# Summing the expert output biases on GpSimd, with logits in column tiles, gathers by pairs and the flag inside the stream

## The chip, the cores, the metric

The kernel runs on one core of one Trainium2 chip, in fp32. The metric is the device time in microseconds of one execution; medians of several executions are given. Every execution quoted here counted as fast (undisturbed).

PE is TensorE, PEld its weight loads, DVE VectorE, ACT ScalarE, POOL GpSimd. The traces name a program line with L; lines move a little from kernel to kernel. The granted clock is the share of its full clock that PE was given; 0.50 is called half rate. Tiles that start with ps lie in PSUM: psh is the output of an expert's first or second layer, psy of a combine, psr holds the routing logits, pswt the transposed routing weights, psbo the biases, pss the window attention's logits, psa a gather; psrt and lgT belong to the changed logits, wbe and wb to the changed biases, pw holds the window weights.

## The reference, cut to what matters

The input has 32 x 128 tokens of 256 channels. Layer 0 is attention over all tokens; layer 1 is a windowed attention (24 neighbours) and a mixture of eight experts, all of them used for every token and weighted by a softmax:

```python
def _L1_ffn_ref(x, Wr, br, W1, ..., W2, ..., Wo, bo):
    feat = jnp.mean(x, axis=0)
    w = jax.nn.softmax(feat @ Wr + br, axis=-1)              # routing weights, tokens x 8
    h = jnp.einsum('bfd,edh->bfeh', x, W1) + b1
    h = jax.nn.relu(_bn(h, g1, be1, m1, v1))
    h = jnp.einsum('bfeh,ehk->bfek', h, W2) + b2
    h = jax.nn.relu(_bn(h, g2, be2, m2, v2))
    y = jnp.einsum('bfeh,ehd->bfed', h, Wo) + bo             # bo: 8 x 256
    return jnp.einsum('bfed,fe->bfd', y, w)                  # so sum_e w_e * bo_e is added
```

## The kernel before

Layer 1 is one hand-ordered stream (the scheduler keeps the program's order on every engine). A "piece" is the matmuls of an expert's first layer, of its second layer, or of a combine; there are 193, one per slot. The side work of a group of four token tiles (one block of 512 tokens; eight groups) is put into slots between the pieces, and a new group starts every 24 slots (one period). In each slot VectorE's, ScalarE's and GpSimd's steps (the `POSTS`) are issued first, then TensorE's side steps, then the piece. Two PSUM banks (`ps_x`) serve all side steps in turn.

```python
        def gather(i, early=False):                    # window-weighted sum of tile i
            acc = bank(f"psa{i}", early)[:, : D + 1]
            nc.tensor.matmul(acc, lhsT=pws[i][:, EDGE : EDGE + P], rhs=xl[:, i % NRING, :], ...)
            if i:                                      # 32 rows of the tile before
                nc.tensor.matmul(acc[:EDGE], lhsT=pws[i - 1][P - EDGE :, EDGE + P :],
                                 rhs=xl[P - EDGE :, (i - 1) % NRING, :], ...)
            if i + 1 < NTILE:                          # 32 rows of the tile after
                nc.tensor.matmul(acc[P - EDGE :], lhsT=pws[i + 1][:EDGE, :EDGE],
                                 rhs=xl[:EDGE, (i + 1) % NRING, :], ...)
        # ... cut ...
        def route(b, early=False):                     # routing logits: 8 columns out
            ...
            for r in range(TPB):
                for c in range(2):
                    nc.tensor.matmul(lg[:, r, :], lhsT=xfT[:, c, r * P : (r + 1) * P],
                                     rhs=Wr[:, c, :], start=(c == 0), stop=(c == 1))
        # ... routed, route_exp, route_norm: the softmax on VectorE and ScalarE, cut ...
        def turn_routes(b):                            # weights, transposed: 8 rows
            ps = bank(f"pswt{b}", False)
            for r in range(TPB):
                nc.tensor.transpose(ps[:E, r * P : (r + 1) * P], blk[b][1][:, r, :], ident)
        # ... turned_routes: VectorE copies them to wT, cut ...
        def biases(b):                                 # sum_e w_e * bo_e as 8-row matmuls
            for r2 in range(TPB // 2):
                ps = bank(f"psbo{b}_{r2}", False)
                for k in range(2):
                    r = 2 * r2 + k
                    nc.tensor.matmul(ps[:, k * D : (k + 1) * D],
                                     lhsT=wT[:, r * P : (r + 1) * P], rhs=bo, start=True, stop=True)
        def biased(b):                                 # VectorE adds them to the tokens
            for r2, ps in enumerate(banks.pop(("b", b))):
                t = h1[b * TPB // 2 + r2]
                nc.vector.tensor_tensor(t, t, ps.rearrange("p (k d) -> p k d", k=2), op=ALU.add)
        # ... cut: the slots of one group ...
            put(26, route, g); put(27, routed, g); put(28, route_exp, g); put(29, route_norm, g)
            put(31, turn_routes, g); put(32, turned_routes, g)
            put(34, biases, g); put(35, biased, g)
        # ... cut ...
        START = 26                                     # the slot of the first piece
        # ... cut: the stream; after it, with nothing beside them: ...
        in_range(wf, ok, rs1, 1.0e-34, 1.0e17)         # four VectorE steps each
        in_range(wf, ok, G.rearrange("p k c -> p (k c)"), 1.0e-15, 1.0e15)
        nc.tensor.matmul(n_ok, lhsT=ok, rhs=ones_m[:, :1], start=True, stop=True)
        nc.vector.tensor_scalar(flag, n_ok, P - 0.5, None, op0=ALU.is_lt)
```

Every engine then reads the flag and branches: if a check failed, a general kernel does the work again.

## Time and profile before

| | before |
|---|---|
| median | 1620.54 us (1619.7 to 1621.57, 3 executions) |
| profiled execution | span 1620.3 us, mean granted PE clock 0.988 |
| first expert matmul, end of the last combine | 800.7, 1610.2 us |
| PE busy | 1579.3 us, 97% |

In the timeline a row is: start, length, engine, line, operation, output <- inputs, shape, number of instructions, and in square brackets the idle time before it and what ended it. In the view of stretches a row is: stretch, its length, then the busy time (and number of instructions) of PE, PEld, DVE, ACT and POOL, the granted PE clock, the DMA share and GB/s. The timelines are in the prediction. The view of stretches over one period before:

```profile
1114.81:1218.26 103.45, 103.16 (x374) 63.98 (x374) 30.45 (x81) 32.19 (x45) 2.85 (x4) 1.00 0.03 11
```

### The profile page before, as it was taken

What the parts mean: (1) busy time and instruction counts of PE and PEld (TensorE: products, weight loads), DVE (VectorE), ACT (ScalarE), POOL (GpSimd) and SP (SyncE); (2) the same over time, 40 slices, a digit from 0 to 9 for tenths busy, and PEclk for the clock granted to TensorE, in tenths of its full rate; (3) what the DMA queues carried; (4) which work ended last, traced back from release to release, by engine and by line L of the source; (5) the groups of instructions that cost most, each with busy time, mean ns of one, the idle gap of its engine ahead of it and who ended that gap; (6) DMA issues with size and microseconds to landing.
All of it is one profiled execution on the core that took longest, in us unless ns stands there. A gap on an engine that the chain in (4) does not pass through costs nothing.

```text
span 1620.3 us, 20972 instructions
## 1 busy us (share of the span) xinstructions
PE 1579.3 (97%) x8636; PEld 770.1 (48%) x8636; DVE 830.5 (51%) x1117; ACT 810.7 (50%) x1005; POOL 70.5 (4%) x230
## 2 busy tenths in 40 slices
PE   7999999999999999998899999999999999999997
PEld 5663332222222222223565656656656566565654
DVE  4543668888898898998523223233232232323212
ACT  3226778888888888885323322333233232332321
POOL 0002100000000000000100000000000000000000
PEclk9999999999999999999999999999999999999998
DMA  4200000000000000003200000000000000000000
GB/s 115 58 1 16 16 9 15 9 8 8 2 8 9 1 8 8 1 8 119 71 1 0 26 1 13 14 0 27 0 8 19 1 14 0 0 14 0 14 0 15
DMA packets 30251, 26.58 MB, mean 16 GB/s; under 512 B 7818, under 2 KB 28168, under 8 KB 30148
## 3 DMA queue, kind: packets, MB, share of 16 engines
q1 hardware_dynamic: 28600, 23.68, 5.1%
q10 hardware_dynamic: 1548, 1.48, 0.4%
q8 instruction: 70, 1.15, 0.3%
q14 instruction: 33, 0.27, 0.1%
HBM read 20.71 MB, written 4.44 MB: 16 GB/s over the span
## 4 chain that ended last, share of the span: by engine, by line
PE 96%; DVE 2%; ACT 1%; DMA 0%; issue 0%; ACTq 0%; DVEq 0%
PE psh L1746 28%; PE s L1232 19%; PE av L1269 16%; PE psy L1771 14%; PE z L1254 3%; PE psk L1078 2%; PE pso L1415 2%; PE psk L1489 2%; PE psv L1104 2%; PE psq L1119 2%; PE pss L1514 1%; PE psa L1563 1%; PE psr L1616 1%; PE psa L1558 1%; PE psbo L1667 1%; PE ptf L1599 0%
## 5 line engine op out<-in xcount | busy, mean ns | idle before, releaser
L1241 ACT ACTIVATE pt<-s 128x1024 f32<-128x1024 f32 (+2 forms) x576 | 515.9, 951 | 113.0 <-PE s L1232 102.9
L1284 DVE TENSOR_TENSOR pt<-pt,pt 128x2048 f32<-128x2048 f32 x210 | 481.1, 2291 | 24.6 <-PE av L1269 4.6
L1754 ACT ACTIVATE h<-psh,bshift,bscale 128x512 f32<-128x512 f32 x256 | 198.8, 777 | 551.9 <-PE psh L1746 551.9
L1232 PE MATMUL s<-QT,KT 32*128 32x512 f32 (+3 forms) x2304 | 338.2, 606 | 3.0 <-ACT pt L1241 2.2
L1780 DVE SCALAR_TENSOR_TENSOR h<-psy,w,h 128x256 f32<-128x256 f32 x256 | 112.1, 480 | 407.8 <-PE psy L1771 407.8
L1269 PE MATMUL av<-pt,V 128*32 128x512 f32 (+3 forms) x2304 | 286.9, 570 | 0.0
L1746 PE MATMUL psh<-xfT,W_sb 128*128 128x512 f32 x512 | 238.6, 610 | 0.0
L1771 PE MATMUL psy<-Wo_sb,h 128*128 128x256 f32 x1024 | 233.1, 380 | 0.4 <-ACT h L1754 0.4
L1746 PE MATMUL psh<-h,W_sb 128*128 128x512 f32 x512 | 231.9, 595 | 0.0
L1232 PEld LDWEIGHTS s<-QT,KT 32*128 32x128 f32 x2304 | 117.8, 183 | 227.1 <-issue 118.5
L1771 PEld LDWEIGHTS psy<-Wo_sb,h 128*128 128x128 f32 x1024 | 192.6, 190 | 41.1 <-ACT h L1754 10.0
L1746 PEld LDWEIGHTS psh<-xfT,W_sb 128*128 128x128 f32 x512 | 97.2, 195 | 115.6 <-issue 115.2
L1746 PEld LDWEIGHTS psh<-h,W_sb 128*128 128x128 f32 x512 | 95.4, 190 | 100.3 <-issue 97.6
L1269 PEld LDWEIGHTS av<-pt,V 128*32 128x32 f32 x2304 | 46.9, 108 | 195.5 <-issue 181.2
L1254 PE MATMUL z<-pt,ones_m 128*32 128x512 f32 (+3 forms) x624 | 61.9, 469 | 2.2 <-DVE pt L1284 2.2
L1246 POOL MEMSET pt<- 64x256 f32 x64 | 19.9, 311 | 646.8 <-ACT pt L1241 569.5
L907 POOL TENSOR_TENSOR xr<-xr,outb 128x512 f32<-128x512 f32 x16 | 20.2, 1270 | 493.5 <-DMA xr<-in_x_dram 454.2
L1291 DVE COPY ctx<-av 128x512 f32<-128x512 f32 x16 | 11.1, 691 | 59.1 <-PE av L1269 59.1
L1415 PE MATMUL pso<-woT,big_t 128*128 128x256 f32 x128 | 33.4, 411 | 5.1 <-DVE big_t L1325 5.1
L1254 PEld LDWEIGHTS z<-pt,ones_m 128*32 128x32 f32 x624 | 18.6, 110 | 31.5 <-issue 23.0
L1677 DVE TENSOR_TENSOR h<-h,psbo 128x512 f32<-128x512 f32 x16 | 11.0, 688 | 44.0 <-PE psbo L1667 44.0
L1489 PE MATMUL psk<-big_t,Ksb 128*128 128x256 f32 x128 | 30.6, 381 | 2.4 <-ACT big_t L1470 2.4
(150 smaller groups left out, 830.5 us busy)
## 6 DMA issues: line engine op xcount, KB each, us to landing
xg<-in_x_dram SPq DMA_DIRECT2D x32, 128.0 KB
xr<-in_x_dram SPq DMA_DIRECT2D x16, 256.0 KB
W_sb<-in_L_ffn_W_dram SPq DMA_DIRECT2D x16, 256.0 KB
out_dram<-h SPq DMA_DIRECT2D x16, 256.0 KB
rec<-rd SPq DMA_DIRECT2D x60, 64.0 KB
Wo_sb<-in_L_ffn_Wo_dram SPq DMA_DIRECT2D x8, 256.0 KB
in_w_n<-in_L_conv_in_w_dram ACTq DMA_DIRECT2D x1, 512.0 KB
wq_n<-in_L_conv_wq_dram ACTq DMA_DIRECT2D x1, 256.0 KB
```

The lines of the kernel that those rows point to most:

```text
L1078: nc.tensor.matmul(ps, lhsT=wKT[:, c, m * P : (m + 1) * P], rhs=hT[:, c, :], start=(c == 0), stop=(c == 1),)
L1232: nc.tensor.matmul(s[hh // 2][:, hh % 2, lo:], lhsT=KT[rows, g, i * P : (i + 1) * P], rhs=QT[rows, g, b * BLK + lo : (b + 1) * BLK], start ...
L1241: nc.scalar.activation(pt[:, 2 * hp : 2 * hp + 2, lo:], s[hp][:, :, lo:], AF.Exp, scale=SCALE)
L1254: nc.tensor.matmul(zs_ps[k][HD * hh : HD * (hh + 1), lo:], lhsT=ones_m[:, :HD], rhs=pt[:, hh, lo:], start=start, stop=stop,)
L1269: nc.tensor.matmul(avs[k][HD * hh : HD * (hh + 1), lo:], lhsT=V[:, i, (4 * g + hh) * HD : (4 * g + hh + 1) * HD], rhs=pt[:, hh, lo:], star ...
L1284: nc.vector.tensor_tensor(accs[k], accs[k], pt, op=ALU.add)
L1415: nc.tensor.matmul(ps[:, r * D : (r + 1) * D], lhsT=big_t[:, c, n * P : (n + 1) * P], rhs=woT[:, c, :], start=(c == 0), stop=(c == 1),)
L1489: nc.tensor.matmul(ps[:, m * 2 * P : (m + 1) * 2 * P], lhsT=Ksb[:, c, m * P : (m + 1) * P], rhs=big_t[:, c, 2 * q * P : 2 * (q + 1) * P], ...
L1746: nc.tensor.matmul(ps, lhsT=W[name][:, e, c, m * P : (m + 1) * P], rhs=src[:, c, :], start=(c == 0), stop=(c == 1),)
L1754: nc.scalar.activation(dst[:, m, :], ps, AF.Relu, bias=bshift[:, m, k : k + 1], scale=bscale[:, m, k : k + 1],)
L1771: nc.tensor.matmul(ps[:, k, :], lhsT=ht[:, c, r * P : (r + 1) * P], rhs=W["Wo"][:, e, c, :], start=(c == 0), stop=(c == 1),)
L1780: nc.vector.scalar_tensor_tensor(out=h1[q][:, k, :], in0=ps[:, k, :], scalar=w[:, r, e : e + 1], in1=h1[q][:, k, :], op0=ALU.mult, op1=ALU ...
```

## The change

The intent is to take work off PE, which bounds layer 1, and give it to engines with room. (1) The biases are summed on GpSimd: a multiply of 8 x 256 values per token by the weights, then three adds. (2) The logits are made transposed, in four 32-column tiles at a time, copied by ScalarE and turned by one transpose; the stream therefore starts two slots later. (3) Two tiles are gathered in one go, full matmuls first and edge matmuls after. (4) Checks and flag move into the stream. (5) The first output projections do what is ready first.

```diff
-        bo = wf.tile([E, D], F32, name="bo")
+        bo = wf.tile([P, E, D], F32, name="bo")              # on every partition
...
+            order = [(q, 0, 0) for q in qs]                      # project_out
+            for q in qs:
+                order += [(q, 0, 1), (q, 1, 0), (q, 1, 1)]
...
-        def gather(i, early=False):
+        def gather(i0, early=False):
+            two = (i0, i0 + 1)
+            for i in two:
+                ... the full matmul of i
+            for i in two:
+                ... the edge matmuls of i
...
-            for r in range(TPB):
-                for c in range(2):
+            for c in range(2):
+                for r in range(TPB):
                     nc.tensor.matmul(
-                        lg[:, r, :],
-                        lhsT=xfT[:, c, r * P : (r + 1) * P],
-                        rhs=Wr[:, c, :],
+                        ps[32 * r : 32 * (r + 1), :P],
+                        lhsT=Wr[:, c, :],                        # 8 columns, padded to 32
+                        rhs=xfT[:, c, r * P : (r + 1) * P],
...
+        def copy_route(b):
+            nc.scalar.copy(lgT, banks.pop(("r", b))[:, :P])
+        def turn_route(b):
+            nc.tensor.transpose(ps[:, :P], blk[b].pop(), ident)
...
-        (turn_routes, turned_routes, biases)
+        def bias_sum(b, r):
+            w = blk[b][1]
+            t = fx.tile([P, E, D], F32, tag="wbe", name=f"wbe{b}_{r}", bufs=1)
+            nc.gpsimd.tensor_tensor(
+                t, bo, w[:, r, :].unsqueeze(2).to_broadcast([P, E, D]), op=ALU.mult
+            )
+            nc.gpsimd.tensor_tensor(t[:, :4], t[:, :4], t[:, 4:], op=ALU.add)
+            nc.gpsimd.tensor_tensor(t[:, :2], t[:, :2], t[:, 2:4], op=ALU.add)
+            nc.gpsimd.tensor_tensor(blk[b][2][:, r, :], t[:, 0], t[:, 1], op=ALU.add)
...
+            put(26, route, g); put(27, copy_route, g); put(28, turn_route, g)
+            put(29, routed, g); put(30, route_exp, g); put(31, route_norm, g)
+            for r in range(TPB):
+                put(32 + 4 * r, bias_sum, g, r)
+            put(50, biased, g)                                   # adds blk[b][2] from SBUF
+            if g == NGRP - 1:
+                put(40, in_bounds); put(42, count_ok); put(43, set_flag)
...
-        START = 26
+        START = 28
```

More of the change, by code (lines that the diff above doesn't have):

```diff
@@ L875, in short @@
     Ksb = const.tile([P, 2, D], F32, name="Ksb")
-    Wr = const.tile([P, 2, E], F32, name="Wr")
+    Wr = const.tile([P, 2, 32], F32, name="Wr")
+    nc.gpsimd.memset(Wr, 0.0)
     br = const.tile([P, E], F32, name="br")
@@ L1137, in short @@
             nc.sync.dma_start(out=abias, in_=row(ins["L1_attn_bias"]).to_broadcast([P, 1]))
-            nc.sync.dma_start(out=Wr, in_=ins["L1_ffn_Wr"].rearrange("(c p) e -> p c e", p=P))
+            nc.sync.dma_start(out=Wr[:, :, :E], in_=ins["L1_ffn_Wr"].rearrange("(c p) e -> p c e", p=P))
             nc.sync.dma_start(out=br, in_=row(ins["L1_ffn_br"]).to_broadcast([P, E]))
@@ L1389, in short @@
                 )
-        bo = wf.tile([E, D], F32, name="bo")
-        nc.sync.dma_start(out=bo, in_=ins["L1_ffn_bo"])
+        bo = wf.tile([P, E, D], F32, name="bo")
+        nc.sync.dma_start(out=bo[:, :1], in_=ins["L1_ffn_bo"][:1].unsqueeze(0).to_broadcast([P, 1, D]))
+        nc.sync.dma_start(out=bo[:, 1:], in_=ins["L1_ffn_bo"][1:].unsqueeze(0).to_broadcast([P, E - 1, D]))
         h1, kts, pws, blk, banks = {}, {}, {}, {}, {}
@@ L1407, in token, with project_out @@
             return h1[n // 2][:, n % 2, :]
-        def project_out(q, early=False):
-            ps = bank(f"pso{q}", early)
-            for r in range(2):
-                n = 2 * q + r
-                for c in range(2):
-                    nc.tensor.matmul(
-                        ps[:, r * D : (r + 1) * D],
-                        lhsT=big_t[:, c, n * P : (n + 1) * P],
-                        rhs=woT[:, c, :],
-                        start=(c == 0),
-                        stop=(c == 1),
-                    )
-            banks["o", q] = ps
+        def project_out(*qs, early=False):
+            for q in qs:
+                banks["o", q] = bank(f"pso{q}", early)
+            order = [(q, 0, 0) for q in qs]
+            for q in qs:
+                order += [(q, 0, 1), (q, 1, 0), (q, 1, 1)]
+            for q, r, c in order:
+                n = 2 * q + r
+                nc.tensor.matmul(
+                    banks["o", q][:, r * D : (r + 1) * D],
+                    lhsT=big_t[:, c, n * P : (n + 1) * P],
+                    rhs=woT[:, c, :],
+                    start=(c == 0),
+                    stop=(c == 1),
+                )
         def residual(q):
@@ L1554, in windowed @@
                 nc.vector.tensor_tensor(pt[:, t, k], pt[:, t, k], w, op=ALU.mult)
-        def gather(i, early=False):
-            acc = bank(f"psa{i}", early)[:, : D + 1]
-            nc.tensor.matmul(
-                acc, lhsT=pws[i][:, EDGE : EDGE + P], rhs=xl[:, i % NRING, :],
-                start=True, stop=False, skip_group_check=True,
-            )
-            if i:
+        def gather(i0, early=False):
+            two = (i0, i0 + 1)
+            for i in two:
+                acc = bank(f"psa{i}", early)[:, : D + 1]
+                banks["a", i] = acc
                 nc.tensor.matmul(
-                    acc[:EDGE], lhsT=pws[i - 1][P - EDGE :, EDGE + P :],
-                    rhs=xl[P - EDGE :, (i - 1) % NRING, :], start=False, stop=False,
-                    skip_group_check=True,
-                )
-            if i + 1 < NTILE:
-                nc.tensor.matmul(
-                    acc[P - EDGE :], lhsT=pws[i + 1][:EDGE, :EDGE],
-                    rhs=xl[:EDGE, (i + 1) % NRING, :], start=False, stop=True,
-                    skip_group_check=True,
-                )
-            banks["a", i] = acc
+                    acc, lhsT=pws[i][:, EDGE : EDGE + P], rhs=xl[:, i % NRING, :],
+                    start=True, stop=False, skip_group_check=True,
+                )
+            for i in two:
+                acc = banks["a", i]
+                if i:
+                    nc.tensor.matmul(
+                        acc[:EDGE], lhsT=pws[i - 1][P - EDGE :, EDGE + P :],
+                        rhs=xl[P - EDGE :, (i - 1) % NRING, :], start=False, stop=False,
+                        skip_group_check=True,
+                    )
+                if i + 1 < NTILE:
+                    nc.tensor.matmul(
+                        acc[P - EDGE :], lhsT=pws[i + 1][:EDGE, :EDGE],
+                        rhs=xl[:EDGE, (i + 1) % NRING, :], start=False, stop=True,
+                        skip_group_check=True,
+                    )
         def gathered(i):
@@ L1608, in expert_turned, with route @@
             blk[b] = [xfT]
-        def route(b, early=False):
+        def route(b):
             xfT = blk[b][0]
-            ps = bank(f"psr{b}", early)
-            lg = ps[:, : TPB * E].rearrange("p (r e) -> p r e", e=E)
-            for r in range(TPB):
-                for c in range(2):
+            ps = bank(f"psr{b}", False)
+            for c in range(2):
+                for r in range(TPB):
                     nc.tensor.matmul(
-                        lg[:, r, :],
-                        lhsT=xfT[:, c, r * P : (r + 1) * P],
-                        rhs=Wr[:, c, :],
+                        ps[32 * r : 32 * (r + 1), :P],
+                        lhsT=Wr[:, c, :],
+                        rhs=xfT[:, c, r * P : (r + 1) * P],
                         start=(c == 0),
@@ L1622, in route @@
                     )
-            banks["r", b] = lg
+            banks["r", b] = ps
+        def copy_route(b):
+            lgT = fx.tile([P, P], F32, tag="lgT", name=f"lgT{b}", bufs=1)
+            nc.scalar.copy(lgT, banks.pop(("r", b))[:, :P])
+            blk[b].append(lgT)
+        def turn_route(b):
+            ps = bank(f"psrt{b}", False)
+            nc.tensor.transpose(ps[:, :P], blk[b].pop(), ident)
+            banks["r", b] = ps[:, :P].rearrange("p (r e) -> p r e", r=TPB)[:, :, :E]
         def routed(b):
@@ L1647, in route_norm @@
             )
-        def turn_routes(b):
-            ps = bank(f"pswt{b}", False)
-            for r in range(TPB):
-                nc.tensor.transpose(ps[:E, r * P : (r + 1) * P], blk[b][1][:, r, :], ident)
-            banks["w", b] = ps
-        def turned_routes(b):
-            wT = fx.tile([E, BLK], F32, tag="wT", name=f"wT{b}", bufs=1)
-            nc.vector.tensor_copy(wT, banks.pop(("w", b))[:E])
-            blk[b].append(wT)
-        def biases(b):
-            wT = blk[b][2]
-            pss = []
-            for r2 in range(TPB // 2):
-                ps = bank(f"psbo{b}_{r2}", False)
-                for k in range(2):
-                    r = 2 * r2 + k
-                    nc.tensor.matmul(
-                        ps[:, k * D : (k + 1) * D], lhsT=wT[:, r * P : (r + 1) * P], rhs=bo,
-                        start=True, stop=True,
-                    )
-                pss.append(ps)
-            banks["b", b] = pss
@@ L1674, in biased @@
-        def biased(b):
-            for r2, ps in enumerate(banks.pop(("b", b))):
+        def bias_sum(b, r):
+            w = blk[b][1]
+            if r == 0:
+                blk[b].append(fx.tile([P, TPB, D], F32, tag="wb", name=f"wb{b}"))
+            t = fx.tile([P, E, D], F32, tag="wbe", name=f"wbe{b}_{r}", bufs=1)
+            nc.gpsimd.tensor_tensor(
+                t, bo, w[:, r, :].unsqueeze(2).to_broadcast([P, E, D]), op=ALU.mult
+            )
+            nc.gpsimd.tensor_tensor(t[:, :4], t[:, :4], t[:, 4:], op=ALU.add)
+            nc.gpsimd.tensor_tensor(t[:, :2], t[:, :2], t[:, 2:4], op=ALU.add)
+            nc.gpsimd.tensor_tensor(blk[b][2][:, r, :], t[:, 0], t[:, 1], op=ALU.add)
@@ L1676, in biased, with in_bounds, count_ok @@
+        def biased(b):
+            for r2 in range(TPB // 2):
                 t = h1[b * TPB // 2 + r2]
                 nc.vector.tensor_tensor(
-                    t, t, ps.rearrange("p (k d) -> p k d", k=2), op=ALU.add
+                    t, t, blk[b][2][:, 2 * r2 : 2 * r2 + 2, :], op=ALU.add
                 )
+        def in_bounds():
+            in_range(wf, ok, rs1, 1.0e-34, 1.0e17)
+            in_range(wf, ok, G.rearrange("p k c -> p (k c)"), 1.0e-15, 1.0e15)
+        def count_ok():
+            n_ok = bank("n_ok", False)
+            nc.tensor.matmul(n_ok[:1, :1], lhsT=ok, rhs=ones_m[:, :1], start=True, stop=True)
+            banks["n"] = n_ok
@@ L1682, in short, with set_flag @@
+        def set_flag():
+            nc.vector.tensor_scalar(
+                flag, banks.pop("n")[:1, :1], P - 0.5, None, op0=ALU.is_lt
+            )
         PERIOD = 3 * E
@@ L1716, in steps @@
                 put(14 + k, windowed, js)
-            for k in range(TPB):
+            for k in range(0, TPB, 2):
                 put(16 + k, gathered, i0 + k)
+                put(16 + k, gathered, i0 + k + 1)
                 put(15 + k, gather, i0 + k)
@@ L1724, in steps @@
             put(26, route, g)
-            put(27, routed, g)
-            put(28, route_exp, g)
-            put(29, route_norm, g)
-            put(31, turn_routes, g)
-            put(32, turned_routes, g)
-            put(34, biases, g)
-            put(35, biased, g)
+            put(27, copy_route, g)
+            put(28, turn_route, g)
+            put(29, routed, g)
+            put(30, route_exp, g)
+            put(31, route_norm, g)
+            for r in range(TPB):
+                put(32 + 4 * r, bias_sum, g, r)
+            put(50, biased, g)
+            if g == NGRP - 1:
+                put(40, in_bounds)
+                put(42, count_ok)
+                put(43, set_flag)
             return out
@@ L1736, in short @@
             root, centre, keys_tile, expert_input, expert_turned, routed, route_exp,
-            route_norm, turned_routes, biased,
+            route_norm, copy_route, bias_sum, biased, in_bounds, set_flag,
         }
@@ L1808, in head @@
             qs, jss = group(0)
-            for q in qs:
-                project_out(q, True)
+            project_out(*qs, early=True)
             keys_tile(0)
@@ L1835, in head @@
                 windowed(js)
+            for i in range(0, TPB, 2):
+                gather(i, True)
             for i in range(TPB):
-                gather(i, True)
-                if i:
-                    gathered(i - 1)
-            gathered(i)
+                gathered(i)
             root(0, TPB, mean2, rstd2)
@@ L1864, in short @@
         assert not plan
-        in_range(wf, ok, rs1, 1.0e-34, 1.0e17)
-        in_range(wf, ok, G.rearrange("p k c -> p (k c)"), 1.0e-15, 1.0e15)
-    with tc.tile_pool(name="fl", bufs=1) as flp, tc.tile_pool(
-        name="ps_f", bufs=1, space=PSUM
-    ) as ps_f:
-        n_ok = ps_f.tile([1, 1], F32, name="n_ok")
-        nc.tensor.matmul(n_ok, lhsT=ok, rhs=ones_m[:, :1], start=True, stop=True)
-        nc.vector.tensor_scalar(flag, n_ok, P - 0.5, None, op0=ALU.is_lt)
 @with_exitstack
```

## The prediction

> **What bounds the kernel now.** I read the page first (busy shares, the chain that ended last), then TensorE's own timeline over one period of layer 1, then the waits, then the last microseconds.
>
> ```profile
> PE 1579.3 (97%) x8636; PEld 770.1 (48%) x8636; DVE 830.5 (51%) x1117; ACT 810.7 (50%) x1005; POOL 70.5 (4%) x230
> PE 96%; DVE 2%; ACT 1%; DMA 0%; issue 0%; ACTq 0%; DVEq 0%
> ```
>
> PE is busy 97% and carries 96% of the chain; GpSimd (POOL) is busy 4%. From about 800 us on, layer 1 is one PE stream: 193 expert "pieces" (two layers and a combine per expert and block), with the side work of the token groups between them. Any PE time taken out there shortens the span, provided no wait takes its place. The timeline of PE shows what each side step costs, if one reads start to start (the second column overstates it, because ends overlap):
>
> ```profile
> 1109.53 3.60 PE L1746 MATMUL psh<-xfT,W_sb 128*128 128x512 f32 x8
> 1112.96 1.85 PE L1616 MATMUL psr<-Wr,xfT 128*128 128x8 f32 x16
> 1114.67 3.70 PE L1771 MATMUL psy<-Wo_sb,h 128*128 128x256 f32 x16
> 1118.20 3.60 PE L1746 MATMUL psh<-h,W_sb 128*128 128x512 f32 x8
> ...
> 1132.84 0.60 PE L1652 MATMUL pswt<-ident,w 128*8 128x128 f32 x4
> 1133.27 3.60 PE L1746 MATMUL psh<-xfT,W_sb 128*128 128x512 f32 x8
> ...
> 1143.61 3.60 PE L1746 MATMUL psh<-h,W_sb 128*128 128x512 f32 x8
> 1147.14 1.13 PE L1667 MATMUL psbo<-bo,wT 8*128 8x256 f32 x4
> 1148.55 1.13 PE L1667 MATMUL psbo<-bo,wT 8*128 8x256 f32 x4 [0.29 <-ACT kt L1501]
> 1149.61 3.70 PE L1746 MATMUL psh<-xfT,W_sb 128*128 128x512 f32 x8
> 1153.15 1.46 PE L1514 MATMUL pss<-kt,big_t 128*128 128x192 f32 x8
> ...
> 1169.52 0.60 PE L1558 MATMUL psa<-xl,pw 128*128 128x257 f32 x2
> 1170.05 0.40 PE L1563 MATMUL psa<-xl,pw 32*32 32x257 f32 x1
> 1170.05 0.40 PE L1569 MATMUL psa<-xl,pw 32*32 32x257 f32 x1
> 1170.29 0.38 PE L1563 MATMUL psa<-xl,pw 32*32 32x257 f32 x1
> 1170.30 0.38 PE L1569 MATMUL psa<-xl,pw 32*32 32x257 f32 x1
> 1170.60 3.70 PE L1746 MATMUL psh<-h,W_sb 128*128 128x512 f32 x8
> ```
>
> An undisturbed piece is 3.44 us (1118.20 to 1121.64 in the same timeline). Logits cost 1.71, the turn of the weights 0.43, the biases 2.47, one gather 1.08. The pieces after psr, psbo and psa take 3.53 to 3.54, and the one before psbo 3.53: about 0.1 us for each change of array shape, charged to a neighbour. A whole period is 103.45 us: 24 pieces at 3.44, and 20.7 of side work.
>
> The granted clock of three stretches, from the view of stretches:
>
> ```profile
> 1041.80:1045.21 3.41, 3.12 (x11) 1.81 (x11) 1.32 (x2) 1.25 (x2) 0.00 (x0) 1.00 0.00 0
> 1045.21:1048.63 3.42, 3.42 (x5) 1.35 (x4) 0.05 (x1) 0.78 (x1) 0.00 (x0) 0.50 0.00 0
> 1147.61:1151.02 3.41, 3.12 (x12) 1.58 (x11) 1.38 (x2) 0.89 (x2) 0.00 (x0) 1.00 0.00 0
> ```
>
> A stretch that holds all of a group's psbo (1042.00 to 1044.47) is followed by 3.41 us at clock 0.50; one that holds only part of it is not.
>
> **What the Trainium skill says.** "TensorE: Matmul & The Clock Gate", Part 1, describes a free-running window of 3413 ns after which an inactive array falls to half rate. The trace agrees: 3.41 us at 0.50. That an 8-row matmul counts as inactive is my inference from these stretches. "TensorEngine Tiling (Array Packing)", Key Properties: a change of tiling mode drains TensorE; the 0.1 us above is that. "SBUF — State Buffer", Who interferes with whom: a VectorE instruction with two SBUF inputs, or in a 2-port mode, and a GpSimd instruction that reads SBUF block each other for a whole instruction. The trace agrees: beside the 1.27 us adds on POOL, a VectorE tensor_tensor with both inputs in SBUF took 0.92 us at 801.54 (usually 0.19), while one with PSUM and SBUF took 0.16 at 801.13, unharmed. "GPSIMD Engine Reference", 3.1, gives 4497 ns for a 2048-element fp32 tensor_tensor; the trace has only the 512-element one.
>
> **The change, part by part.**
> 1. *Biases off PE.* psbo: 2.47 + 0.19 of shape changes = 2.66 us in the six groups with the wait; in the other two 1.92 + 0.19 = 2.11. Sum 6 x 2.66 + 2 x 2.11 = 20.2 us. pswt: 8 x 0.43 = 3.5 us. Their VectorE copy goes too, which was beside PE anyway.
> 2. *The half-rate stretches that psbo causes.* Four in this trace (837, 1045, 1253, 1359 us), each makes a piece 5.23 instead of 3.54: 1.7 us. The profiled execution took 1622.08 against the median 1620.54, about one more than usual, so I take 3.5: 5.9 us.
> 3. *Logits in column tiles.* 16 instructions again, but four tiles of 32 columns at once. The attention has that form: eight 128-column instructions start within 0.22 us (753.54 to 753.76), so sixteen 0.44; plus three shape terms of 0.1; plus one transpose of 0.11 (pst: 0.43 for four). 0.85 instead of 1.71 + 0.1: saves 0.95 a group. In the first group nothing is saved: the stream now starts two slots later, so nothing lies between the logits, ScalarE's copy and the transpose; I put 0.8 us of waiting there, which eats it. 7 x 0.95 = 6.6 us.
> 4. *Gathers by pairs.* Two now: 2 x (1.08 + 0.1) = 2.36. A pair: four full instructions 0.86, a change 0.1, four rounds of edge tiles 3 x 0.24 + 0.31, 0.1 in the next piece: 2.09. Saves 0.27 a pair, two pairs in seven groups: 3.8 us. In the head VectorE is the limit there: nothing.
> 5. *The end.* Last combine ends on VectorE at 1610.19, then the range checks, a matmul and the flag until 1612.82; flag read, branch and program end take 7.4 us more. With the flag set earlier VectorE can read it at 1610.2: saves 2.6 us. The same work in the stream costs PE 0.3.
> 6. *Head.* The first output projections now do the half of the contraction that is ready while PE waits 5.1 us for big_t. VectorE gets its second tile six half-rate matmuls after the first rather than eight: 0.9 us.
> 7. *GpSimd.* Per token tile a multiply of 2048 elements and adds of 1024, 512, 256. Scaled by 1.27 us per 512: 5.1 + 2.5 + 1.3 + 0.6 = 9.5 us, 38 a group, out of a period near 99. It has room, and the result is wanted seven slots later. Loading bo on all partitions is 1 MB; at the 119 GB/s of the page's slice, about 9 us. It delays the x tiles that landed at 776.5, which are wanted at 797.5: hidden.
>
> Sum: 20.2 + 3.5 + 5.9 + 6.6 + 3.8 + 2.6 + 0.9 - 0.3 = 43.2 us. Off this I take 2 us for new waits (next part): 1620.5 - 41.2 = 1579 us, 2.6% less.
>
> **The rivals.**
> - *The port lock reaches PE.* The window multiply on VectorE has two SBUF inputs and falls among the 38 us of GpSimd work. Today it ends at 1164.8 for a gather at 1169.52. The new start shifts the pieces by two slots, so it now queues behind a combine: I count 1.1 us after the combine, with the gather 3.44 after it, some 1.8 us of slack against a lock of up to 5 us. I place it around 31 us after GpSimd's start near -1, in the fourth tile's multiply or first add, waiting 0.5 to 2 us. For it: the 0.92 above. Against: VectorE is 30% busy here and wins the port between two GpSimd instructions. If every group lost 2.7 us: +19, or 1596. Combines read PSUM and one SBUF tensor, so they should not block; if they do, 1600.
> - *The half rate returns elsewhere.* The new edge rounds (1.03 us) or column tiles could be counted as idle, as psbo was. Against: psr's 1.7 us of nearly empty array never triggered it. If it did, 1585.
> - *GpSimd becomes the bound.* It would have to take over 99 us a group, 2.6 times my figure. Unlikely.
> - *No path through PE.* If the stream were held by VectorE or ScalarE, only the end would gain: 1617. The busy rows (VectorE 30, ScalarE 32 of 103 us a period) speak against it.
>
> **Range and chances.** Parts 1 and 2 alone (29.6 us) give 1591; everything without new waits and with four half-rate stretches saved gives 1576. A better packing than my shape terms could bring 1570; lost waits end near 1596. So 1579, range 1568 to 1596. The 2% line is 1588: faster 0.78, same 0.21, slower 0.01.
>
> **What would show it.** Right: no psbo and pswt; periods near 98.9 us (103.45 - 2.66 - 0.43 - 0.95 - 0.54); sixteen psr instructions within 0.5 us; pairs with four 32x257 rounds before the next piece; no clock of 0.50 after 800 us; GpSimd near 40% busy in layer 1 and out of the chain; about 7.5 us from the last combine to the end. Wrong: PE idle before psa with VectorE's window multiply as releaser, combines well over 0.48 us, or a period above 101 us.

## The result

The changed kernel took 1575.78 us (median of 4, 1572.53 to 1578.83) against 1620.28 us for the kernel before (median of 4). The ratio is 0.9724, 95% interval 0.9702 to 0.9746: 2.8% faster. Ratios here are the mean time of one kernel's fast runs over that of the other's in the same rounds, so not quite the ratio of the medians quoted. In a later set of executions it was 1573.82 us and 0.9707. The prediction was 1579, range 1568 to 1596.

The same page parts of the changed kernel, busy shares and the chain by engine:

```profile
PE 1542.2 (98%) x8548; PEld 750.1 (48%) x8548; DVE 843.3 (53%) x1109; ACT 812.7 (52%) x1013; POOL 327.1 (21%) x359
...
PE 93%; DVE 5%; ACT 1%; DMA 1%; issue 0%; ACTq 0%; SPq 0%; DVEq 0%
```

PE still bounds; it does 37 us less. GpSimd went from 70 to 327 us and is not in the chain. (The 5% of VectorE is largely its adds in the attention, which this view now puts in the chain; the change does not touch them.)

The view of stretches gives one period of layer 1, 24 pieces and a group's side work:

```profile
993.53:1092.34 98.81, 98.81 (x363) 61.37 (x362) 31.64 (x81) 32.39 (x46) 34.95 (x19) 1.00 0.04 11
```

98.81 us where it was 103.45 (or 105.14, with a half-rate stretch), PE busy for all of it, clock 1.00. PE's timeline for the new side steps:

```profile
992.89 0.64 PE L1627 MATMUL psr<-xfT,Wr 128*32 128x128 f32 x16
993.46 3.70 PE L1775 MATMUL psh<-h,W_sb 128*128 128x512 f32 x8
997.00 3.60 PE L1775 MATMUL psh<-xfT,W_sb 128*128 128x512 f32 x8
1000.43 0.27 PE L1643 MATMUL psrt<-ident,lgT 128*128 128x128 f32 x1
1000.54 3.62 PE L1800 MATMUL psy<-Wo_sb,h 128*128 128x256 f32 x16
...
1045.32 1.03 PE L1568 MATMUL psa<-xl,pw 128*128 128x257 f32 x4
1046.29 0.40 PE L1575 MATMUL psa<-xl,pw 32*32 32x257 f32 x1
1046.29 0.40 PE L1581 MATMUL psa<-xl,pw 32*32 32x257 f32 x1
1046.53 0.38 PE L1575 MATMUL psa<-xl,pw 32*32 32x257 f32 x1
...
1047.27 3.70 PE L1775 MATMUL psh<-xfT,W_sb 128*128 128x512 f32 x8
```

Logits take 0.57 us start to start and the transpose 0.11; a pair of gathers 1.95. GpSimd's timeline, one tile's multiply and its first two adds:

```profile
1035.95 3.60 POOL L1676 TENSOR_TENSOR wbe<-bo,w 128x2048 f32<-128x2048 f32 x1
1039.63 2.36 POOL L1679 TENSOR_TENSOR wbe<-wbe 128x1024 f32<-128x1024 f32 x1
1042.06 1.26 POOL L1680 TENSOR_TENSOR wbe<-wbe 128x512 f32<-128x512 f32 x1
```

And VectorE's timeline at the same time, with the window multiply (L1560):

```profile
1042.09 0.88 DVE L1809 SCALAR_TENSOR_TENSOR h<-psy,w,h 128x256 f32<-128x256 f32 x2 [0.85 <-PE psy L1800]
1042.88 1.86 DVE L1560 TENSOR_TENSOR pw<-pw,window 128x384 f32<-128x384 f32 x2
```

Two combines run beside the GpSimd add at their usual 0.88 us. The two window multiplies take 1.86 us together where two take 1.1: the first, begun at 1042.88, took 0.86 us, across the end of the 1.26 us add at 1043.32; the second took 1.08 us beside GpSimd's last add, which itself took 0.92 us where it usually takes 0.72. Yet the second gather of the pair starts on time, and PE has no idle time before psa in layer 1.

### The profile page after: what moved, and what is told of

The parts are those of the page before. It is cut to its first block, busy times and chain, and to the rows that moved or that the text cites.

```text
span 1577.1 us, 20929 instructions
## 1 busy us (share of the span) xinstructions
PE 1542.2 (98%) x8548; PEld 750.1 (48%) x8548; DVE 843.3 (53%) x1109; ACT 812.7 (52%) x1013; POOL 327.1 (21%) x359
## 4 chain that ended last, share of the span: by engine, by line
PE 93%; DVE 5%; ACT 1%; DMA 1%; issue 0%; ACTq 0%; SPq 0%; DVEq 0%
PE psh L1775 28%; PE s L1234 18%; PE av L1271 15%; PE psy L1800 14%; DVE pt L1286 4%; PE z L1256 3%; PE psk L1080 2%; PE pso L1422 2%; PE psk L1495 2%; PE psv L1106 2%; PE psq L1121 2%; PE pss L1520 1%; PE psa L1575 1%; PE psa L1568 1%; PE ptf L1610 1%; PE pt L1071 0%
## 5 line engine op out<-in xcount | busy, mean ns | idle before, releaser
L1775 PE MATMUL psh<-xfT,W_sb 128*128 128x512 f32 x512 | 231.0, 594 | 0.0
L1676 POOL TENSOR_TENSOR wbe<-bo,w 128x2048 f32<-128x2048 f32 x32 | 115.3, 3602 | 238.9 <-DVE w L1666 237.0
L909 POOL TENSOR_TENSOR xr<-xr,outb 128x512 f32<-128x512 f32 x16 | 20.2, 1270 | 300.3 <-DMA xr<-in_x_dram 220.8
L1679 POOL TENSOR_TENSOR wbe<-wbe 128x1024 f32<-128x1024 f32 x32 | 75.3, 2352 | 2.5
L1680 POOL TENSOR_TENSOR wbe<-wbe 128x512 f32<-128x512 f32 x32 | 40.7, 1273 | 2.5
```

The lines of the kernel that those rows point to most:

```text
L1676: nc.gpsimd.tensor_tensor(t, bo, w[:, r, :].unsqueeze(2).to_broadcast([P, E, D]), op=ALU.mult)
L1679: nc.gpsimd.tensor_tensor(t[:, :4], t[:, :4], t[:, 4:], op=ALU.add)
L1775: nc.tensor.matmul(ps, lhsT=W[name][:, e, c, m * P : (m + 1) * P], rhs=src[:, c, :], start=(c == 0), stop=(c == 1),)
```

## Experiments

Because the total hides terms that cancel, I read from each trace the time from the first expert matmul to the end of the last combine ("layer time") and the half-rate stretches (clock 0.50) within it.

| kernel | median us | ratio to before | layer time | half-rate stretches |
|---|---|---|---|---|
| before | 1620.5 | 1 | 809.51 | 4 |
| changed | 1575.8 | 0.9724 | 768.22 | 0 |
| e1 biases alone | 1589.06 | 0.9807 | 778.98 | 0 |
| e2 logits alone | 1627.05 | 1.0035 | 817.69 | 5 |
| e3 pairs alone | 1612.05 | 0.9953 | 801.73 | 2 |
| e4 flag alone | 1616.38 | 0.9971 | 808.14 | 3 |
| e5 8-row matmuls added | 1625.75 | 1.0030 | 815.65 | 6 |
| e6 128-row matmuls added | 1605.98 | 0.9899 | 795.85 | 0 |
| e7 GpSimd work added early | 1582.77 | 0.9763 | 776.25 | 0 |
| e8 the same, later | 1573.86 | 0.9715 | 768.22 | 0 |
| e9 three fillers | 1572.36 | 0.9701 | 768.22 | 0 |
| e10 changed again | 1573.82 | 0.9707 | 768.22 | 0 |
| e11 logits alone, biases later | 1602.87 | 0.9892 | 792.75 | 0 |
| e12 two fillers | 1570.68 | 0.9686 | 768.22 | 0 |

All of them were correct. The layer time comes from one profiled execution each, the median from all: the profiled executions of the changed kernel, e3 and e6 were among their kernel's slower ones (e3's took 1617.97 us, where five of its eight lie near 1611.5), by what happens before layer 1 (see Scatter); e2's was its slowest too. My theory was the sum of the prediction; the rivals were that the half rate comes from shape changes or waits, that GpSimd's work reaches PE through VectorE, and that parts of the sum are not additive.

### One part at a time (e1 to e4)

**e1**: only the biases, on the kernel before (its own slots: sums at 30, 34, 38 and 42, addition at 48; START stays 26).

```diff
-            put(31, turn_routes, g); put(32, turned_routes, g)
-            put(34, biases, g); put(35, biased, g)
+            for r in range(TPB):
+                put(30 + 4 * r, bias_sum, g, r)
+            put(48, biased, g)
```

> The kernel before with only the biases moved to GpSimd. My sum: psbo 20.2 and pswt 3.5 us off TensorE, and the half-rate stretches after psbo gone (1.7 us each, 3 to 4 of them): about 29 us less, 1591; the clock is full from about 800 us on. Rival A (the half rate comes from TensorE's changes of shape or waits in general, not from psbo): only 24 us less, 1596, and some stretches of clock 0.50 stay. Rival B (GpSimd's work delays VectorE until TensorE waits): above 1600.

Measured 1589.06 us, 0.9807 (0.9792 to 0.9823). The period is 100.34 us, 3.11 less, where I had 2.66 + 0.43; the layer time falls by 30.5 us, which is 23.7 for the matmuls and transposes and 6.8 for four half-rate stretches. This is some 70% of the whole gain. Rival A falls, as no stretch at half rate is left although the shape changes around psa remain, and so does B: PE does not wait for this work anywhere in layer 1. One period of e1:

```profile
1000.78:1101.12 100.34, 100.34 (x362) 62.46 (x362) 29.49 (x80) 32.22 (x45) 34.69 (x19) 1.00 0.03 11
```

**e2**: only the logits, START 28, the biases left at slots 34 and 35.

> The kernel before with only the logits in column tiles and the start two slots later. My sum: 0.95 us in each of seven groups, nothing in the first: 6.6 us less, 1613.7; psbo and its half-rate stretches stay. Rival (the transpose and its copy cost a wait in every group, 0.5 us or more): 1617 to 1620.

Measured 1627.05 us, 1.0035 (1.0023 to 1.0048): the gain I expected became a loss. PE's timeline of e2:

```profile
1041.60 1.12 PE L1678 MATMUL psbo<-bo,wT 8*128 8x256 f32 x4
1043.01 1.13 PE L1678 MATMUL psbo<-bo,wT 8*128 8x256 f32 x4 [0.29 <-ACT kt L1502]
1044.07 3.72 PE L1784 MATMUL psy<-Wo_sb,h 128*128 128x256 f32 x16
1049.44 1.54 PE L1515 MATMUL pss<-kt,big_t 128*128 128x192 f32 x8 [1.65 <-DVE h L1688]
```

With the start two slots later, the piece after psbo is a combine. VectorE runs its steps in the program's order, and the addition of the biases (L1688) comes after the combine's four steps, which wait for PE: in this trace it begins at 1048.62, as they end; and the attention's logits (pss) need the bank which that addition reads. 7 waits, 11.6 us: a wait that the later start creates and that the rest of the change does not have, because its biases need no bank. The layer time is 8.2 us longer: 11.6 of waits and 1.7 for one more half-rate stretch, less 6.4 for the logits (see e11), make 6.9; the other 1.3 us I did not trace.

**e11** tests this: the same kernel, with the biases' matmuls at slot 38 and the addition at 39.

```diff
-            put(34, biases, g)
-            put(35, biased, g)
+            put(38, biases, g)
+            put(39, biased, g)
```

> The logits alone again, with the biases' matmuls four slots later (their addition on VectorE too). The first version's trace shows TensorE waiting 11.6 us in seven groups before the attention logits, for the bank that the addition of the biases has to read first; that addition now queues behind a combine, since the start moved by two slots. If that wait is the whole loss: it goes, 6.6 us of logits and some 3 us of psbo's own waits are saved, 1611 give or take the half-rate stretches (1.7 us each). If the column tiles or the transpose are themselves dear: still 1618 or more.

Measured 1602.87 us, 0.9892 (0.9873 to 0.9911). The waits before pss are gone. The layer time is 16.8 us shorter than before, which the pieces explain: the period is 101.99 = 103.45 - 0.55 (psbo without its wait) - 0.91 (logits), so 6.4 us for the logits in seven groups and 3.3 in six for psbo, plus four half-rate stretches (6.8): 16.5 of the 16.8. I had expected 1611; most of the 8 us between is those stretches, which also vanished. This tells something about their cause: psbo in one go (1.92 us) does not set them off.

**e3**: only the pairs.

> The kernel before with only the gathers by pairs. My sum: 0.27 us a pair, two pairs in seven groups: 3.8 us less, 1616.5. Rival (the cost of a gather is its rounds of edge tiles and not the change of shape): the same time within 1 us, 1620.

Measured 1612.05 us, 0.9953 (0.9937 to 0.9969). More than expected, but not by the gathers: the period is 102.82, 0.63 less, 4.4 us in seven groups; the other 3.4 of the 7.8 us in this trace are two half-rate stretches that did not fall after a psbo this time. Edge rounds after the first start 0.21 us apart rather than my 0.24.

**e4**: only checks and flag in the stream, at slots 40, 42 and 43 of the last group.

> The kernel before with only the checks and the flag inside the stream. By the prediction 2.6 less 0.3 us: 2.3 us less, 1618. The changed kernel's trace shows 5.9 us from the end of the last combine to the program's end where it was 10.1, so 4.1 less 0.3: 3.8 us less, 1616.5. A rival, that the end is set by the output's transfer: no gain, 1620.

Measured 1616.38 us, 0.9971 (0.9959 to 0.9982). From the end of the last combine to the end of the program this trace has 5.0 us, the trace before 10.1. In the five traces with the flag after the stream this end took 7.8 to 10.1 us; in the nine with it inside, 5.0 to 5.9. So the gain is some 2 to 5 us, of which the checks and the flag that no longer follow the last combine are 2.6. The rest varies between executions; the traces show no counted instruction there, and I did not settle what it depends on.

### The half rate (e5, e6)

Both add eight useless matmuls (sixteen instructions) at slot 34 of each group to the changed kernel, with the same operands but for the number of rows:

```diff
+        def filler(g):
+            for h in range(2):
+                ps = bank(f"fill{g}_{h}", False)
+                for k in range(4):
+                    nc.tensor.matmul(ps[:, (k % 2) * D : (k % 2 + 1) * D],
+                        lhsT=woT[:n, 0, :P], rhs=Ksb[:n, 0, :], start=True, stop=True)   # n = 8 or 128
```

> The changed kernel with eight useless matmuls (sixteen instructions of 256 columns) of 8 rows into two banks in every group, at the slot where the biases were. If few rows make the array count as inactive: 3.45 us of matmuls, 0.3 of wait, 0.2 of shape changes a group, and a half-rate stretch of 3.4 us after most of them, 1.7 us each: 8 x 3.95 + 8 x 1.7 = 45 us over the changed kernel, 1621. Rival (the wait or the change of shape triggers it, or nothing does): the same as with 128 rows but for 1.6 us of shape changes.

> The same useless matmuls with 128 rows. If few rows are the cause: 8 x 3.75 = 30 us over the changed kernel, 1606, and no clock of 0.50 after the head. If the wait for the second bank is the cause: half-rate stretches as with 8 rows, 1619 or so.

Measured 1625.75 us with 8 rows and 1605.98 with 128. With 128 rows the layer time grows by 27.6 us, that is 8 x 3.45 and nothing else (the wait I had allowed for did not occur). With 8 rows it grows by 47.4 us. The filler of one group in e6, on PE's timeline and in the view of stretches:

```profile
1135.29 3.62 PE L1694 MATMUL fill<-Ksb,woT 128*128 128x256 f32 x16
...
1137.78:1141.19 3.41, 3.41 (x18) 3.00 (x17) 0.52 (x2) 0.00 (x0) 3.33 (x2) 1.00 0.00 0
```

The view of stretches of e5:

```profile
1135.33:1138.74 3.41, 3.41 (x15) 2.48 (x14) 0.00 (x0) 1.25 (x2) 3.17 (x4) 1.00 0.00 0
1138.74:1145.57 6.83, 6.83 (x18) 4.92 (x17) 0.88 (x2) 0.00 (x0) 6.59 (x4) 0.50 0.00 1
```

And its PE timeline across the same moment:

```profile
1135.89 4.44 PE L1694 MATMUL fill<-Ksb,woT 8*128 8x256 f32 x16
1140.26 6.33 PE L1810 MATMUL psy<-Wo_sb,h 128*128 128x256 f32 x16
```

PE counts as busy for all of 1135.33 to 1138.74, most of it with 8-row matmuls, and the clock then falls to 0.50 for 6.83 us; the following combine takes 6.33 us instead of 3.62. So matmuls with few rows can count as inactive even while the profile counts PE as busy. A wait for the bank is not needed for it: in neither run does the view of waits show PE waiting at a filler. Six stretches sum to 34.1 us at half rate, 17 us lost, and shape changes 8 x 0.2: 18.7 of the 19.8 us between the two. The kernel before fits, and so do the other kernels with psbo. I laid the clock's 3.41 us stretches over the 40 psbo of the traces of the kernel before, e2, e3, e4 and e11: every stretch that held 2.20 us or more of one (with its wait, 2.47 in all) was followed by half rate, 14 in number; none that held 2.02 or less was, psbo without the wait (1.92) included. (The prediction said that a stretch must hold all of it: in its own trace those before 837 and 1359 us held 2.29 and 2.38.) Whether a psbo falls into one stretch or across two decides, and the stretches do not keep step with the groups. In e5, where the fillers ran on for 1.52 us or more into the half-rate stretch (four groups), a second one followed. Of a low column count nothing is shown: no run of it is as long as psbo.

### The port lock (e7, e8)

The port lock is the prediction's first rival: VectorE and GpSimd holding each other up over SBUF. Both runs add one GpSimd instruction per group to the fourth tile's sum, a multiply of bo by ones; e7 after the add of 1024, e8 after the last add.

```diff
+        def long_add(b):
+            v = bo.rearrange("p e (h d) -> p (e h) d", d=P)
+            nc.gpsimd.tensor_tensor(
+                v, v, ones_m.unsqueeze(1).to_broadcast([P, 2 * E, P]), op=ALU.mult)
```

> The changed kernel with one more GpSimd instruction per group (2048 elements, two SBUF inputs, 3.6 to 4.6 us, values unchanged), placed in the fourth tile's sum after the add of 1024, so that it starts about when VectorE is ready for the window multiply (at 1042.1 in the changed kernel's trace). If the port lock holds VectorE for the whole instruction: the window multiply ends at about 1046.3 to 1047.3 where the second gather of the pair wants it at 1045.9, so TensorE waits 0.4 to 1.4 us in each of seven groups: 3 to 10 us more than the changed kernel. If the two can share: no more than 1 us.

> The same added GpSimd instruction after the fourth tile's last add, when the window multiplies are done. If only the moment matters (the lock) and not the amount of GpSimd work: the changed kernel's time within 1 us. If the amount matters: as slow as with the instruction earlier.

Measured 1582.77 us for e7 (0.9763) and 1573.86 for e8 (0.9715). Timelines of GpSimd, VectorE and PE in e7:

```profile
1041.44 4.52 POOL L1672 TENSOR_TENSOR bo<-bo,ones_m 128x2048 f32<-128x2048 f32 x1
...
1042.38 5.54 DVE L1560 TENSOR_TENSOR pw<-pw,window 128x384 f32<-128x384 f32 x2
...
1046.52 0.67 PE L1568 MATMUL psa<-xl,pw 128*128 128x257 f32 x2 [1.11 <-DVE pw L1560]
```

The first window multiply is held until the 4.52 us instruction ends at 1045.96 (it takes 4.00 us), and PE waits in six groups, 6.6 us by the view of waits; the period grows by 1.34 us. The same instruction two steps later costs nothing (layer time 768.22, as without it). So the lock is real, and it is luck that what runs at this moment in the changed kernel is a short add: the prediction expected a multiply or the first add there.

### A better version (e9, e12; e10 is the changed kernel again)

With the cause known, I filled PE's waits outside the stream with full-size useless matmuls. e9: three (128 x 512) after the first attention scores, eight between the first output projections, seven before the first expert transposes. e12 leaves out the eight.

```diff
                     held.append((*u, scores(*u)))
+                    if u == units[0]:
+                        fz = ps_z.tile([P, BLK], F32, tag="z", name="fill_z")
+                        for _ in range(3):
+                            nc.tensor.matmul(fz, lhsT=woT[:, 0, :P], rhs=QT[:, 0, :BLK],
+                                             start=True, stop=True)
...
             expert_input(0)
+            warm(7)          # seven full matmuls of 256 columns into a combine bank
             expert_turn(0, True)
```

> The changed kernel with useless full-size matmuls where TensorE waits: three after the first attention scores, eight between the first output projections, seven before the first expert transposes. In the changed kernel's trace half-rate stretches begin at 126.8, 765.1 and 795.8 us. If a busy array keeps the clock: they go, about 1.7 us of the 5.7 us that TensorE works in the last one, 1 to 2 us in the head, up to 2 us at the attention's start: 3 to 5 us less, about 1572. If TensorE is not what those stretches wait for (VectorE's and ScalarE's chains are): no gain, or a loss of up to 2 us.

> The changed kernel again, on the same chip as the one with useless matmuls, to compare them: 0.9724 of the kernel before, 1575.8 us, spread of some 6 us between executions.

> The changed kernel with useless matmuls only after the first attention scores and before the first expert transposes, not between the output projections. The fuller version's trace shows 1.6 us less in the attention's start and a new half-rate stretch in the head, from 783.0 us, during the useless matmuls. If those between the output projections only moved the stretch: now the one before the transposes goes as well, 3 us less than the changed kernel, 1571. If the head is set by VectorE's chain: about 1.6 us less, 1572.

Measured: e10 1573.82 us (1572.65 to 1574.33), e9 1572.36, e12 1570.68 (1569.59 to 1571.11). e9 missed its 3 to 5 us: its eight matmuls kept the clock up early in the head, but a half-rate stretch came at 783.0 instead, into the gathers and the seven matmuls. These then ran until 791.16, 1.0 us after the tile that the expert transposes wait for was ready (790.14), so the filler itself held the head up. e12 is the fastest of all: from the first attention scores to the first expert matmul its trace has 675.6 us where e10 has 678.9. None of its five executions overlaps e10's, though the two ratios' intervals (0.9670 to 0.9702, and 0.9694 to 0.9720) touch; they were not timed in the same rounds, nor on the same chip. PE's timeline of the attention's start in e12:

```profile
120.41 2.84 PE L1347 MATMUL fill_z<-QT,woT 128*128 128x512 f32 x6
123.18 2.52 PE L1234 MATMUL s<-QT,KT 32*128 32x384 f32 x16
125.64 1.06 PE L1271 MATMUL av<-pt,V 128*32 128x512 f32 x8
```

In e10 the first av group took 1.94 us at half rate; here it takes 1.06.

## Why the prediction was right

- **Bound.** PE alone set layer 1, before and after: PE is busy for 98.81 of 98.81 us of the period, and the predicted period was 98.9.
- **The sum.** 43.2 us less 2 for waits was forecast (41.2 of 1620.5 is 2.5%, not the 2.6% written), 44.5 measured. Mechanism and size both held; the terms that were mis-sized are named below, and they partly cancel.
- **Biases off PE.** Predicted 23.7 us (20.2 + 3.5), measured 23.7 in e1.
- **Half rate.** Predicted 5.9 us (3.5 stretches), 6.8 with the four of the trace; gone in the changed kernel. The inference that few rows count as inactive is shown by e5 and e6; that all of a psbo must lie in one stretch was not right, 2.20 us were enough. How many fall in an execution of the kernel before is chance: its trace and those of e2 to e4 have 2 to 5.
- **Logits.** Predicted 6.6 us, measured 6.4 within e11. That the part needs the rest of the change was not in the prediction: alone it loses (e2), as its later start turns the biases' addition into a wait of PE.
- **Pairs.** Predicted 3.8 us, measured 4.4 in e3: the edge rounds were sized at 0.24 us and are 0.21.
- **End.** Predicted 2.6 us; the profiled execution shows 4.1 (10.1 to 5.9), and other traces 2 to 5. The prediction's own sign was about 7.5 us from the last combine to the end; the trace has 5.9. The 2.6 are the work moved; what the rest is stays open.
- **Head.** Predicted 0.9 us. From the first scores to the first expert matmul the six traces with the old order have 680.3 to 683.8 us, the six with the new one and no fillers in the head 678.9 to 681.6. They overlap, and no run has this part alone; not shown.
- **New waits.** I took off 2 us; the measured waits on PE in the layer time are nil (the first transpose of the logits waits 0.44 us just before it, where the prediction allowed 0.8), and this is most of why the result came out below 1579. The rival was real, e7 shows it, but by my estimate from e7 (4.52 us, of which PE waited 1.11) it needs an instruction above about 3.4 us that starts at that moment. The multiply was mis-sized as well: 5.1 us predicted, 3.60 measured, so a group takes GpSimd 33 us rather than 38, and the window multiply met the 1.26 us add: luck, not plan. Combines do not block, as said: 0.88 us a pair beside GpSimd's work. This is the better evidence; the prediction's example with a PSUM input (0.16 us at 801.13) began 0.01 us before the add beside it.
- **Shape changes.** The 0.1 us terms came out, but that all of them are drains of a tiling mode is not shown: before, 0.1 us follows psr too, whose matmuls are 128*128 like the pieces around it.
- **Together.** In the layer time, 23.7 + 6.8 + 6.4 + 4.4 = 41.3, less 0.3 for the flag's matmul, against 41.3 between the two traces. The parts add up to 0.3 us once each is read without its side effects.
- **Scatter.** The changed kernel's own executions lie 6 us apart. In its slower, profiled execution the first attention scores start at 122.8 us, against 119.3 in e10. In that trace a longer half-rate phase in the prologue makes the difference: its 128x128 transposes between 20 and 24 us take 0.42 us each, those of e10 0.27. The traces of e3 and e6 have the same long phase (first scores at 123.9 and 123.5), the other eleven do not (119.0 to 120.3). The phase of the clock's windows at the kernel's start is my reading of it, not tested.

## What to carry to other kernels

Look at what a small side matmul does to the array beyond its own time: the change of shape (here 0.1 us on each side) and above all a run of matmuls with few rows, after which this kernel ran at half rate for 3.4 us, in e5 for up to 6.8. Work moved to GpSimd was free here, as it had room and no VectorE instruction with two SBUF inputs that PE waits for started beside one of its long instructions; place the long ones, not only count them. And measure parts alone with their side effects read out of the trace: here a good part (logits) looked like a loss, because moving it put another step into a queue behind a combine.

## What the Trainium skill lacked or had wrong

- "TensorE: Matmul & The Clock Gate": it says that the monitor watches how busy PE is, not that busy time as the profile counts it can count as idle. Sixteen instructions of 8 rows, with PE busy 3.41 of 3.41 us, led to a clock of 0.50; the same with 128 rows did not (e5, e6). A window need not be idle altogether: 2.20 us of an 8-row run with its wait in 3.41 us was enough (e3), 2.02 was not (e2).
- "GPSIMD Engine Reference", section 3.1: 4497 ns for an fp32 tensor_tensor of 2048 elements. A multiply whose second operand repeats one value for 256 elements took 3602 ns; the one in e7, whose second operand repeats a block of 128 values, took 4.52 us, as the page has it.
- "TensorEngine Tiling (Array Packing)", Key Properties, gives no size for the drain of a mode change: here about 0.1 us at each change, charged to the neighbouring pieces (3.53 to 3.55 us instead of 3.44).
- "SBUF — State Buffer", Who interferes with whom: agrees (e7: a window multiply that usually takes 0.55 us took 4.00 beside a GpSimd instruction of 4.52), nothing to mend.
